# A one-core graph-attention layer with residual norm: the last four row blocks are reordered over five engines

## The chip, the cores and the metric

One core of a Trainium2 chip runs the whole kernel in one launch. The metric is device time in microseconds (us), the median over several runs; lower is better. The engines are called by their full names in the text and by the profile's names in its lines: TensorE (PE, its weight loads PEld), VectorE (DVE), ScalarE (ACT), GpSimd (POOL) and SyncE (SP). A "q" behind an engine's name in a line marks its instruction queue: waits, branches and DMA issues, in which the engine itself doesn't compute.

## The reference, cut to what matters

```python
def gnn(h, adj_mat, W, a):                 # h: 4096x512, adj_mat: 4096x4096, W: 512x2048, a: 4x1024x1
    ht = (h @ W).reshape(N, 4, 512).transpose(1, 0, 2)
    src, dst = einsum('hnd,hd->hn', ht, a_src), einsum('hnd,hd->hn', ht, a_dst)
    e = leaky_relu(src[:, :, None] + dst[:, None, :], 0.01) + adj_mat[None]
    att = softmax(e, axis=-1)
    return einsum('hij,hjd->hid', att, ht).mean(axis=0)

out = layernorm(x + gnn(x, adj, W, a))     # over the 512 columns, no weights, eps 1e-5
```

All data is float32. The entries of `adj` reach 1e9, while the scores from `src` and `dst` are small. So in nearly every row the softmax puts its whole weight on the one column where `adj` is greatest, and a row's attention output is simply that column's row of `x` times the mean of the four head matrices of `W`.

## The kernel before

The kernel uses that fact. `leading_rows` finds the greatest entry of each row of `adj`, gathers the row of `x` that it points to, multiplies it by the mean of the heads, adds the residual and normalises. It also tests for every row whether the greatest entry leads by enough for this to hold, and counts the rows where it does not; the count ends in `any_bad`. If `any_bad` is above zero, a second program part, `general`, works out the doubtful blocks in full. With these inputs it is skipped, but each engine loads `any_bad` and branches on it at its end (L61, L62).

**Tiling.** Rows are taken in NB = 32 blocks of 128. A block of `adj` is 2 MB, loaded through SyncE's DMA queue into one of six buffers. `hold` keeps all 32 blocks of `x` (128 x 32 x 512) and later, in place, the output.

**A block's way.** VectorE reduces the 4096 columns to 128 segment maxima (L163), finds the greatest segment (`find_segment`), GpSimd works out its place (`row`, L174) and gathers the 32 numbers of that segment (`lead`, L176, an indirect DMA); VectorE finds the place in it (`find_column`), GpSimd the column number (`col`, L200) and gathers the row of `x` (`y`, L186). TensorE transposes `y` (`turn`, L213), ScalarE copies it to SBUF (`yt`, L215), TensorE multiplies by `w_sum` in four 128x512 products (`products`, L228). The residual is added by one more product with the identity (`residual`, L221). Each float32 product shows in the trace as two passes. Then the row's mean and variance are taken and the block is normalised into `hold`. For the last block, 31, the segment's gather is used only for the test; its column is found by a search of the whole row (`find_column_in_row`, L206).

**Order.** All engines run in program order; a loop over t = 0 to 31 writes out a software pipeline by hand (column two steps, products three, statistics four behind the load), and a list of calls after it (lines 463 to 525) writes out the tail. Nothing is moved by a scheduler. BEHIND is 24 and LATE is 28. Blocks 0 to 23 are normalised in the loop by ScalarE (`stats`, `finish`) with the reciprocal root on GpSimd (`rstd`). The `x` of blocks 24 to 27 is loaded last, so their products are put by in SBUF (`put_by`) and added to `x` later (`add_x`, L244). Blocks 28 to 31 are measured on VectorE (`moments`: L281, L285, and a root on ScalarE, L287) and normalised by `normalise` (L297); block 31 is done in two halves of 256 columns (`products_of_half` L270, `stats_of_half` L304, `finish_in_halves`).

**The test.** `bound` (four parts, over VectorE, TensorE and ScalarE) makes a limit from the norms, `test` compares (VectorE), `count` sums over partitions by a product with ones (L394), `report` turns the sums into `n_bad` and `any_bad` (three VectorE operations, L398 to L401).

**The stores** go through SyncE's queue in program order: a store waits for its data and for one of eight completion counters to be free, and what follows in the queue waits behind it. Each store reads `hold`.

Of the kernel before, what the change touches and what calls it, by code (L numbers as in the profile page):

```python
# [10 lines left out]
U32 = mybir.dt.uint32  # L11
I32 = mybir.dt.int32
AF = mybir.ActivationFunctionType
OP = mybir.AluOpType
# [6 lines left out]
P = 128  # L21
# [45 lines left out]
def leading_rows(ctx, tc, x, adj, W, a, out, ident, v, n_bad, any_bad):  # L67
# [100 lines left out]
    def find_segment(ib):  # L168
        seg = seg_of.pop(ib)
        nc.vector.max(out=top[:, ib, :], in_=seg)  # L170
        at = small.tile([P, 8], U32, name="at")
        nc.vector.max_index(at, top[:, ib, :], seg)  # L172
        row = small.tile([P, 1], U32, name="row")
        nc.gpsimd.tensor_tensor(row, at[:, 0:1], first[:, ib : ib + 1], op=OP.add)  # L174
        lead = lead_pool.tile([P, E], F32, name="lead")
        nc.gpsimd.indirect_dma_start(  # L176
            out=lead, out_offset=None, in_=adj_segs,
            in_offset=bass.IndirectOffsetOnAxis(ap=row[:, :1], axis=0),
        )
        start = at_of[ib] = small.tile([P, 1], U32, name="start")  # L180
        nc.gpsimd.tensor_tensor(start, at[:, 0:1], width, op=OP.mult)  # L181
        lead_of[ib] = lead

    def gather_rows(ib, col):
        y = y_t[ib] = y_pool.tile([P, D], F32, name="y")
# [5 lines left out]
    def find_inner(ib):  # L191
        nc.vector.max(out=inner[:, ib, :], in_=lead_of[ib])
# [16 lines left out]
    def turn(ib):  # L209
        y = y_t.pop(ib)  # L210
        tp = psum.tile([P, KB, P], F32, name="tp", bufs=2)
        for kb in range(KB):
            nc.tensor.transpose(tp[:, kb, :], y[:, ts(kb, P)], ident)  # L213
        yt = yt_of[ib] = rows.tile([P, KB, P], F32, name="yt")
        nc.scalar.copy(yt, tp)  # L215

    def residual(ib):
        start = ib not in o_ps
        if start:
            o_ps[ib] = psum.tile([P, D], F32, name="o")  # L220
        nc.tensor.matmul(o_ps[ib], ident, hold[:, ib, :], start=start, stop=False)  # L221

    def products(ib, lo=0, hi=KB):
        start = ib not in o_ps
        if start:
            o_ps[ib] = psum.tile([P, D], F32, name="o")
        for kb in range(lo, hi):
            nc.tensor.matmul(  # L228
                o_ps[ib], yt_of[ib][:, kb, :], w_sum[:, kb, :],
                start=(start and kb == 0), stop=(kb == KB - 1),  # L230
            )
# [11 lines left out]
    def add_x(engine, ib):  # L243
        engine.tensor_add(hold[:, ib, :], hold[:, ib, :], o_ps["by"][:, ib - BEHIND, :])  # L244
        o_ps[ib] = hold[:, ib, :]

    def stats(ib):
        o, i = o_ps[ib], slice(ib, ib + 1)
        sq = rows.tile([P, D], F32, name="sq")
        nc.scalar.activation(sq, o, AF.Identity, scale=-1.0 / D, accum_out=nm[:, i])  # L250
        sq = rows.tile([P, D], F32, name="sq")
        nc.scalar.activation(sq, o, AF.Square, bias=nm[:, i], accum_out=sd[:, i])  # L252
# [6 lines left out]
    def finish(ib):  # L259
        i = slice(ib, ib + 1)  # L260
        nc.scalar.activation(hold[:, ib, :], o_ps.pop(ib), AF.Identity, bias=nm[:, i], scale=sd[:, i])  # L261

    def residual_in_halves(ib):
        o_ps[ib] = [psum.tile([P, D // 2], F32, name="o") for _ in range(2)]
        for k, o in enumerate(o_ps[ib]):
            nc.tensor.matmul(o, ident, hold[:, ib, ts(k, D // 2)], start=True, stop=False)
# [10 lines left out]
    def moments(ib):  # L277

        if ib < NB - 1:
            st = small.tile([P, nc.vector.BN_STATS_DIM], F32, name="st", bufs=2)  # L280
            nc.vector.bn_stats(st, o_ps[ib])  # L281
        else:
            st = halves_st
        mv = mean_var[ib] = small.tile([P, nc.vector.BN_AGGR_DIM], F32, name="mv", bufs=3)
        nc.vector.bn_aggr(mv, st)  # L285
        r = rt[ib] = sd[:, ib : ib + 1]
        nc.scalar.activation(r, mv[:, 1:2], AF.Sqrt, bias=eps)  # L287

    def factor(ib, shift=False):
        nc.vector.reciprocal(rt[ib], rt[ib])  # L290
        if shift:
            nc.vector.scalar_tensor_tensor(
                nm[:, ib : ib + 1], mean_var[ib][:, 0:1], -1.0, rt[ib], op0=OP.mult, op1=OP.mult
            )

    def normalise(ib, o, columns=slice(0, D)):
# [15 lines left out]
    def store(queue, lo, n):  # L312
        queue.dma_start(out_rows[:, ds(lo, n), :], hold[:, ds(lo, n), :])
# [78 lines left out]
    def count():  # L392
        pg = psum.tile([1, NB], F32, name="px", bufs=1)
        nc.tensor.matmul(pg, ones[:, 0:1], gap, start=True, stop=True)  # L394
        return pg
# [8 lines left out]
    vectors = [(kb, h) for kb in range(KB) for h in range(H)]  # L404
    vectors_at = {t: 2 if t < 3 else 1 for t in range(1, 15)}
    COLUMN, PROJECT, STATS, FINISH = 2, 3, 4, 6

    for t in range(NB):
        if t == NB // 2:
            tc.mark_branch_hint_location("general", engines=HINTED)  # L410
        if t in x_at:
            load_x(*x_at[t])
        if t + AHEAD == NB - 1:
            load_x(LATE, Q)
        load_adj(t + AHEAD)
        middle = 1 if t == NB - 1 else 2
        segment_maxima(t, 0, middle)
        if t >= COLUMN:
            find_column(t - COLUMN)
        segment_maxima(t, middle, PIECES)  # L420
        pair = FINISH <= t < BEHIND + FINISH and t % 2 == 0
        if pair:
            rstd(slice(t - FINISH, t - FINISH + 2))
        if t == NB - 1:
            for ib in (BEHIND, BEHIND + 2):
                load_x(ib, 2)
        find_segment(t)
        if t < 2:
            mean_of_heads(t)
        elif t == 2:  # L430
            mean_of_heads(2)
            mean_of_heads(3)
        if t == 0:
            turn_a()
        turned = [(*vectors[0], turn_w(*vectors.pop(0))) for _ in range(vectors_at.get(t, 0))]
        if t == 16:
            head_norms()
        ib = t - PROJECT
        if t == NB - 1:
            for late in range(LATE, NB):  # L440
                row_norm(late)
            residual(LATE)
            residual(LATE + 1)
        if ib >= 0:
            turn(ib)
            if ib > BEHIND:
                products(ib - 1, KB - 1, KB)
            if ib < BEHIND:
                residual(ib)
        for some in turned:  # L450
            head_vector(*some)
        if ib >= 0:
            products(ib, 0, KB if ib < BEHIND else KB - 1)
        if t >= BEHIND + STATS:
            put_by(t - STATS)
        elif t >= STATS:
            stats(t - STATS)
            row_norm(t - STATS)
        if pair:
            finish(t - FINISH)  # L460
            finish(t - FINISH + 1)

    for ib in range(BEHIND, LATE):
        row_norm(ib)
    for ib in range(0, 2 * Q, Q):
        store(nc.sync, ib, Q)
    for ib in range(2 * Q, BEHIND, 2):
        store(nc.sync, ib, 2)
    find_column(NB - 2)
    add_x(nc.gpsimd, BEHIND)  # L470
    add_x(nc.gpsimd, BEHIND + 1)
    find_column_in_row(NB - 1)
    add_x(nc.gpsimd, BEHIND + 2)
    products(LATE, KB - 1, KB)
    residual_in_halves(NB - 1)
    turn(NB - 3)
    products(NB - 3, 0, KB - 1)
    moments(LATE)
    for ib in range(BEHIND, NB):
        find_inner(ib)  # L480
    bound(0)
    products(NB - 3, KB - 1, KB)
    stats(BEHIND)
    factor(LATE)
    normalise(LATE, o_ps.pop(LATE))
    bound(1)
    turn(NB - 2)
    bound(2)
    add_x(nc.vector, LATE - 1)
    stats(BEHIND + 1)  # L490
    moments(LATE - 1)
    products(NB - 2, 0, 2)
    bound(3)
    test()
    pg = count()
    products(NB - 2, 2, KB - 1)
    stats(BEHIND + 2)
    rstd(slice(BEHIND, BEHIND + 2))
    rstd(slice(BEHIND + 2, BEHIND + 3))
    moments(NB - 3)  # L500
    report(pg)
    turn(NB - 1)
    factor(LATE - 1, shift=True)
    factor(NB - 3)
    normalise(NB - 3, o_ps.pop(NB - 3))
    finish(BEHIND)
    finish(BEHIND + 1)
    products(NB - 2, KB - 1, KB)
    products_of_half(NB - 1, 0)
    products_of_half(NB - 1, 1)  # L510
    nc.vector.tensor_add(hold[:, NB - 2, :], o_ps[NB - 2], hold[:, NB - 2, :])
    o_ps[NB - 2] = hold[:, NB - 2, :]
    moments(NB - 2)
    stats_of_half(NB - 1, 0)
    factor(NB - 2)
    normalise(NB - 2, o_ps.pop(NB - 2))
    finish(BEHIND + 2)
    finish(BEHIND + 3)
    stats_of_half(NB - 1, 1)
    moments(NB - 1)  # L520
    factor(NB - 1, shift=True)
    finish_in_halves(NB - 1)
    for ib, n in ((NB - 4, 1), (NB - 3, 1), (BEHIND, 2), (NB - 2, 1), (BEHIND + 2, 2)):
        store(nc.sync, ib, n)
    store(nc.sync, NB - 1, 1)

# [152 lines left out]
```

## Time and profile before

| what | value |
|---|---|
| median of 3 runs | 236.32 us (236.14 to 236.66) |
| the profiled execution | 236.21 us, of which its span (first to last instruction) is 234.6 us |
| TensorE, VectorE, ScalarE, GpSimd busy | 83%, 80%, 48%, 43% of the span |
| DMA | 97.21 MB, 414 GB/s over the span |
| mean granted TensorE clock | 0.975 |

The span begins with the first and ends with the last instruction; the execution's own time lies 1.6 us above it. The profile cuts the span into 40 slices, follows the work that ended last back as a chain, and lists groups of instructions by line, engine and tile with their durations. Times in the trace's answers are counted from the span's start.

### The profile page before, as it was taken

To read this page: it belongs to the slowest core of one execution; us is meant where nothing else is said; L and a number is where in the kernel's file an instruction comes from. 1 tells how busy PE (TensorE), PEld (TensorE's weight loads), DVE (VectorE), ACT (ScalarE), POOL (GpSimd) and SP (SyncE) were. 2 spreads that over 40 slices of the span, in tenths; PEclk is the share of its full clock that TensorE was granted. 3 is DMA by queue.
4 is the path that set the end of the run, shared out by engine and by line. 5 is a ranking of instruction groups with operands and counts; after the bars stand their busy time and mean duration, and the time that the engine had idled before them with its cause. 6 is when DMAs were issued, how large, how long until landed. Compare 5 with 4: busy or idle time off the path is not lost.

```text
span 234.6 us, 2498 instructions
## 1 busy us (share of the span) xinstructions
PE 195.2 (83%) x683; PEld 101.4 (43%) x683; DVE 188.4 (80%) x302; ACT 111.6 (48%) x267; POOL 101.2 (43%) x215
## 2 busy tenths in 40 slices
PE   0188929999999999999979879797998968698990
PEld 0034514756565655555534333242443423244460
DVE  1736875589869995999589989998799999989672
ACT  2012011255474747474758354646464645166582
POOL 1012232414527462646353645464365464549130
PEclk9999977999999999999999999999799999999998
DMA  6999999999999999999999999999999999999985
GB/s 226 439 428 426 443 425 430 415 440 412 440 420 426 424 437 434 425 424 428 427 432 433 425 433 422 432 418 429 425 432 418 422 425 427 411 425 419 417 355 210
DMA packets 13697, 97.21 MB, mean 414 GB/s; under 512 B 2152, under 2 KB 2664, under 8 KB 7792
## 3 DMA queue, kind: packets, MB, share of 16 engines
q1 hardware_dynamic: 10080, 88.08, 88.9%
q0 software_dynamic: 3584, 8.92, 9.6%
q8 instruction: 6, 0.10, 0.2%
q14 instruction: 11, 0.09, 0.1%
q10 hardware_dynamic: 16, 0.02, 0.0%
HBM read 88.62 MB, written 8.39 MB: 414 GB/s over the span
## 4 chain that ended last, share of the span: by engine, by line
DMA 45%; POOL 17%; issue 15%; PE 10%; DVE 9%; ACT 1%; POOLq 0%; SPq 0%; DVEq 0%
DMA adj_t<-in_adj_dram 42%; DVE seg L163 8%; PE o L228 7%; POOL lead L176 6%; POOL y L186 5%; DMA y<-in_x_dram,col 3%; POOL sd L256 2%; PE o L270 2%; POOL start L181 1%; POOL row L174 1%; POOL col L200 1%; PE tp L213 1%; PE o L221 1%; ACT yt L215 1%; POOL sd L255 1%
## 5 line engine op out<-in xcount | busy, mean ns | idle before, releaser
L163 DVE TENSOR_REDUCE seg<-adj_t 128x64 f32<-128x2048 f32 (+1 forms) x68 | 146.0, 2149 | 32.7 <-DMA adj_t<-in_adj_dram 32.3
L228 PE MATMUL o<-w_sum,yt 128*128 128x512 f32 x248 | 115.1, 605 | 1.7 <-ACT yt L215 1.7
L228 PEld LDWEIGHTS o<-w_sum,yt 128*128 128x128 f32 x248 | 44.5, 191 | 54.8 <-issue 42.3
L215 ACT COPY yt<-tp 128x512 f32<-128x512 f32 x32 | 18.8, 588 | 44.3 <-PE tp L213 44.3
L176 POOL DMA_INDIRECT lead<-in_adj_dram,row x32 | 32.3, 1010 | 15.5 <-POOL row L174 15.0
L186 POOL DMA_INDIRECT y<-in_x_dram,col x32 | 30.9, 965 | 15.4 <-POOL col L200 15.2
L318 PE MATMUL o<-hold,ident 128*128 128x512 f32 x32 | 18.9, 745 | 17.5 <-DMA hold<-in_L_gnn_W_dram 17.5
L213 PE MATMUL tp<-ident,y 128*128 128x128 f32 x128 | 20.0, 280 | 12.6 <-DMA y<-in_x_dram,col 12.6
L221 PE MATMUL o<-hold,ident 128*128 128x512 f32 x52 | 27.3, 611 | 0.0
L213 PEld LDWEIGHTS tp<-ident,y 128*128 128x128 f32 x128 | 14.9, 143 | 25.4 <-issue 25.0
L174 POOL TENSOR_TENSOR row<-at,first 128x1 uint32<-128x1 uint32 x32 | 6.1, 190 | 42.0 <-DVE at L172 42.0
L336 ACT COPY wt<-tp 128x512 f32<-128x512 f32 x16 | 9.2, 587 | 31.4 <-PE tp L334 31.4
L200 POOL TENSOR_TENSOR col<-start,within 128x1 uint32<-128x1 uint32 x31 | 5.9, 190 | 40.1 <-DVE within L198 40.1
L235 ACT ACTIVATE sq<-hold 128x512 f32<-128x512 f32 x32 | 19.8, 619 | 0.0
L342 PEld LDWEIGHTS pv<-at_d,wt 128*128 128x128 f32 x128 | 16.3, 191 | 6.8 <-ACT wt L336 4.0
L318 PEld LDWEIGHTS o<-hold,ident 128*128 128x128 f32 x32 | 7.4, 243 | 26.7 <-POOL row L174 11.0
L319 ACT ACTIVATE w_sum<-o 128x512 f32<-128x512 f32 x4 | 2.4, 598 | 33.9 <-PE o L318 33.9
L261 ACT ACTIVATE hold<-o,nm,sd 128x512 f32<-128x512 f32 x24 | 17.2, 771 | 0.0
L252 ACT ACTIVATE sq<-o,nm 128x512 f32<-128x512 f32 x24 | 16.5, 688 | 0.8
L342 PE MATMUL pv<-at_d,wt 128*128 128x2 f32 x128 | 15.3, 244 | 0.6 <-ACT wt L336 0.6
L250 ACT ACTIVATE sq<-o 128x512 f32<-128x512 f32 x24 | 14.6, 609 | 0.0
L334 PEld LDWEIGHTS tp<-ident,hold 128*128 128x128 f32 x64 | 7.9, 142 | 6.9 <-issue 6.9
(85 smaller groups left out, 139.8 us busy)
## 6 DMA issues: line engine op xcount, KB each, us to landing
adj_t<-in_adj_dram SPq DMA_DIRECT2D x27, 2048.0 KB, 31.3
hold<-in_x_dram SPq DMA_DIRECT2D x7, 1024.0 KB, 33.2
adj_t<-in_adj_dram SPq DMA_DIRECT2D x6, 1024.0 KB, 25.7
out_dram<-hold SPq DMA_DIRECT2D x10, 512.0 KB, 15.2
adj_t<-in_adj_dram SPq DMA_DIRECT2D x8, 512.0 KB
hold<-in_L_gnn_W_dram SPq DMA_DIRECT2D x4, 1024.0 KB
out_dram<-hold SPq DMA_DIRECT2D x2, 1024.0 KB
hold<-in_x_dram SPq DMA_DIRECT2D x2, 512.0 KB, 14.1
```

Source lines behind the costliest of these rows:

```text
L163: nc.vector.tensor_reduce(seg_of[ib][:, ts(k, S // n)], adj_t[ib][:, ts(k, N // n)].rearrange("p (s e) -> p s e", e=E), axis=AX.X, op=OP.max,)
L176: nc.gpsimd.indirect_dma_start(out=lead, out_offset=None, in_=adj_segs, in_offset=bass.IndirectOffsetOnAxis(ap=row[:, :1], axis=0),)
L186: nc.gpsimd.indirect_dma_start(out=y, out_offset=None, in_=x, in_offset=bass.IndirectOffsetOnAxis(ap=col[:, :1], axis=0),)
L213: nc.tensor.transpose(tp[:, kb, :], y[:, ts(kb, P)], ident)
L215: nc.scalar.copy(yt, tp)
L221: nc.tensor.matmul(o_ps[ib], ident, hold[:, ib, :], start=start, stop=False)
L228: nc.tensor.matmul(o_ps[ib], yt_of[ib][:, kb, :], w_sum[:, kb, :], start=(start and kb == 0), stop=(kb == KB - 1),)
L235: nc.scalar.activation(sq, hold[:, ib, :], AF.Square, accum_out=xx[:, ib : ib + 1])
L252: nc.scalar.activation(sq, o, AF.Square, bias=nm[:, i], accum_out=sd[:, i])
L261: nc.scalar.activation(hold[:, ib, :], o_ps.pop(ib), AF.Identity, bias=nm[:, i], scale=sd[:, i])
L318: nc.tensor.matmul(o, ident, hold[:, w_at + kb * H + h, :], start=(h == 0), stop=(h == H - 1))
L342: nc.tensor.matmul(pv[:, kb, h : 2 * H : H], wt[:, k, :], at_d[:, k, h : 2 * H : H], start=(k == 0), stop=(k == KB - 1),)
```

## The change

The tail is written anew; the loop and the arithmetic stay, but for the places named here.

- `find_segment` is split: the part on GpSimd is now `fetch_segment`, and for block 31 it is called after the gather of block 30's `y` and one `add_x`. The `start` of block 31 is not computed.
- Blocks 24 to 26 are normalised on GpSimd from SBUF (`finish_on_chip`), block 27 by ScalarE as before; all four `add_x` are on GpSimd.
- Block 29's residual is no longer a product, but an addition on VectorE (`add_residual`), as block 30's already was.
- On TensorE, the last product of a late block now stands between the transposes of the next and its products, and the residual of block 31 after the first matrix product of `bound`. `count` stands between the two halves of block 31.
- `report` moves from before the transposes of block 31 to after the normalising of block 30.
- `factor` uses `tensor_scalar` with two operations in place of `scalar_tensor_tensor`.
- The stores of blocks 0 to 23 are issued in the order of `HELD`, and those of the last eight blocks in the order 28, 24 and 25, 29, 26 and 27, 30, 31 (before: 28, 29, 24 and 25, 30, 26 and 27, 31).

```diff
+    def fetch_segment(ib):
+        at = at_of.pop(ib)
         row = small.tile([P, 1], U32, name="row")
...
+    def finish_on_chip(ib):
+        i, h = slice(ib, ib + 1), hold[:, ib, :]
+        o_ps.pop(ib)
+        nc.gpsimd.tensor_scalar(h, h, sd[:, i], nm[:, i], op0=OP.mult, op1=OP.add)
+
+    def add_residual(ib):
+        nc.vector.tensor_add(hold[:, ib, :], o_ps[ib], hold[:, ib, :])
+        o_ps[ib] = hold[:, ib, :]
...
+    HELD = ((8, 2), (10, 2), (0, Q), (12, 2), (14, 2), (Q, Q), (16, 2), (18, 2), (20, 2), (22, 2))
...
             residual(LATE)
-            residual(LATE + 1)
...
-    for ib in range(0, 2 * Q, Q):
-        store(nc.sync, ib, Q)
-    for ib in range(2 * Q, BEHIND, 2):
-        store(nc.sync, ib, 2)
+    for ib, n in HELD:
+        store(nc.sync, ib, n)
     find_column(NB - 2)
     add_x(nc.gpsimd, BEHIND)
-    add_x(nc.gpsimd, BEHIND + 1)
+    fetch_segment(NB - 1)
     find_column_in_row(NB - 1)
-    add_x(nc.gpsimd, BEHIND + 2)
+    for ib in (BEHIND + 1, LATE - 1, BEHIND + 2):
+        add_x(nc.gpsimd, ib)
+    turn(NB - 3)
     products(LATE, KB - 1, KB)
+    products(NB - 3, 0, KB - 1)
+    stats(BEHIND)
+    moments(LATE)
+    bound(0)
     residual_in_halves(NB - 1)
-    turn(NB - 3)
-    products(NB - 3, 0, KB - 1)
-    moments(LATE)
-    for ib in range(BEHIND, NB):
+    for ib in range(BEHIND, NB - 1):
         find_inner(ib)
-    bound(0)
-    products(NB - 3, KB - 1, KB)
-    stats(BEHIND)
+    bound(1)
     factor(LATE)
     normalise(LATE, o_ps.pop(LATE))
-    bound(1)
     turn(NB - 2)
+    products(NB - 3, KB - 1, KB)
     bound(2)
-    add_x(nc.vector, LATE - 1)
     stats(BEHIND + 1)
     moments(LATE - 1)
-    products(NB - 2, 0, 2)
+    find_inner(NB - 1)
     bound(3)
     test()
-    pg = count()
-    products(NB - 2, 2, KB - 1)
+    products(NB - 2, 0, KB - 1)
     stats(BEHIND + 2)
     rstd(slice(BEHIND, BEHIND + 2))
+    finish_on_chip(BEHIND)
+    finish_on_chip(BEHIND + 1)
     rstd(slice(BEHIND + 2, BEHIND + 3))
+    finish_on_chip(BEHIND + 2)
+    add_residual(NB - 3)
+    turn(NB - 1)
     moments(NB - 3)
-    report(pg)
-    turn(NB - 1)
     factor(LATE - 1, shift=True)
+    finish(LATE - 1)
     factor(NB - 3)
     normalise(NB - 3, o_ps.pop(NB - 3))
-    finish(BEHIND)
-    finish(BEHIND + 1)
     products(NB - 2, KB - 1, KB)
     products_of_half(NB - 1, 0)
+    pg = count()
     products_of_half(NB - 1, 1)
-    nc.vector.tensor_add(hold[:, NB - 2, :], o_ps[NB - 2], hold[:, NB - 2, :])
-    o_ps[NB - 2] = hold[:, NB - 2, :]
+    add_residual(NB - 2)
     moments(NB - 2)
     stats_of_half(NB - 1, 0)
     factor(NB - 2)
     normalise(NB - 2, o_ps.pop(NB - 2))
-    finish(BEHIND + 2)
-    finish(BEHIND + 3)
+    report(pg)
     stats_of_half(NB - 1, 1)
     moments(NB - 1)
     factor(NB - 1, shift=True)
     finish_in_halves(NB - 1)
-    for ib, n in ((NB - 4, 1), (NB - 3, 1), (BEHIND, 2), (NB - 2, 1), (BEHIND + 2, 2)):
+    for ib, n in ((LATE, 1), (BEHIND, 2), (NB - 3, 1), (BEHIND + 2, 2), (NB - 2, 1)):
         store(nc.sync, ib, n)
     store(nc.sync, NB - 1, 1)
```

More of the change, by code (lines that the diff above doesn't have):

```diff
@@ L170, in find_segment @@
         nc.vector.max(out=top[:, ib, :], in_=seg)
-        at = small.tile([P, 8], U32, name="at")
+        at = at_of[ib] = small.tile([P, 8], U32, name="at")
         nc.vector.max_index(at, top[:, ib, :], seg)
+        if ib < NB - 1:
+            fetch_segment(ib)
+    def fetch_segment(ib):
+        at = at_of.pop(ib)
         row = small.tile([P, 1], U32, name="row")
@@ L179, in find_segment @@
         )
-        start = at_of[ib] = small.tile([P, 1], U32, name="start")
-        nc.gpsimd.tensor_tensor(start, at[:, 0:1], width, op=OP.mult)
         lead_of[ib] = lead
+        if ib < NB - 1:
+            start = at_of[ib] = small.tile([P, 1], U32, name="start")
+            nc.gpsimd.tensor_tensor(start, at[:, 0:1], width, op=OP.mult)
     def gather_rows(ib, col):
@@ L291, in factor @@
         if shift:
-            nc.vector.scalar_tensor_tensor(
-                nm[:, ib : ib + 1], mean_var[ib][:, 0:1], -1.0, rt[ib], op0=OP.mult, op1=OP.mult
+            nc.vector.tensor_scalar(
+                nm[:, ib : ib + 1], mean_var[ib][:, 0:1], rt[ib], -1.0, op0=OP.mult, op1=OP.mult
             )
```

## The prediction, written before the changed kernel had run

> **What bounds the kernel now.** I read the slices first, then the chain in order of time, then the closing lines of the program, because a chain that is followed through data can miss what an engine does after its last computation.
>
> The two rows of the slices (40 of 5.87 us each; a digit is a busy share in tenths):
>
> ```profile
> POOL  1012232414527462646353645464365464549130
> DMA  6999999999999999999999999999999999999985
> ```
>
> The DMA engines are full in every slice but the first and the last two, so up to 223 us only fewer bytes could help, and the change moves none away. What is left to win or lose lies after that. The end of the chain (start, length, what):
>
> ```profile
> 203.44 0.14 issue
> 203.58 0.63 PE tp L213 x4
> ...
> 215.64 0.59 ACT yt L215
> ...
> 220.57 0.59 ACT yt L215
> ...
> 225.69 3.55 PE o L270 x16
> ...
> 230.69 0.56 ACT hold L310
> ```
>
> From the landing of the gather for block 27 (203.44) TensorE sets the pace, with short waits, to 229.24; then 2.0 us of statistics and normalising, the last store is issued at 231.29 and has landed at 233.60.
>
> Now the lines of the branch and the end, from the views of L61, L62 and L674 (durations in ns as min/median/max, then first and last start in us):
>
> ```profile
> L61 POOLq TENSOR_LOAD <-any_bad x1: 508/508/508, 225.2 to 225.2; - x1
> ...
> L62 POOLq INC_SWDGE_SEM  x1: 1476/1476/1476, 226.7 to 226.7; - x1
> ...
> L674 POOLq EVENT_SEMAPHORE  x4: 17/17/17, 233.8 to 234.5; - x4
> L674 POOLq DRAIN  x3: 40/103/5306, 228.2 to 234.3; - x3
> L674 SPq DRAIN  x3: 7/7/7, 233.7 to 234.0; - x3
> ```
>
> This is the part to see. GpSimd, whose last digit is 0, has a closing sequence of its own: it loads `any_bad` (from 225.22), takes the branch, spends 1.48 us on INC_SWDGE_SEM, then 5.31 us in a DRAIN (228.23 to 233.53): **8.31 us from the load to the end of the DRAIN**. SyncE, waiting for the last store, is through at 233.75, and the closing barrier takes 0.8 us from there. So two paths end within 0.2 us of each other, and only one is in the chain. The load needs `any_bad`, which VectorE writes early:
>
> ```profile
> 223.69 0.14 DVE L401 TENSOR_SCALAR any_bad<-total 1x1 int32<-1x1 f32 x1
> ...
> 225.25 0.19 POOL L257 TENSOR_TENSOR nm<-nm,sd 128x1 f32<-128x1 f32 x1
> ```
>
> It had been ready for 1.4 us; GpSimd's own last `rstd` (L257) let the load go.
>
> **What the Trainium skill says.** (1) "Perfetto Trace Analysis", section Sequencer-only Instruction: the profile reports such an instruction from the moment that its semaphores are satisfied to the end of execution, so waiting for a semaphore is not in it. By that, 5.31 us is work. (2) "VectorE: DVE Perf Modes", The DRAIN you can't avoid: closing DRAINs are about 12 ns on all engines. The trace agrees for SyncE (7 ns) and disagrees for GpSimd (5306 ns); the measurement decides. (3) "DMA: Bandwidth & Descriptors", Queues, rings and completion order: on each DMA engine descriptors are consumed in ring order. The trace agrees: the last five stores land in order of issue (229.05, 230.81, 231.41, 232.62, 233.60). (4) "GPSIMD Engine Reference", Elementwise: the best case is 769 ns for 512 elements, more with two inputs. The two-input L244 takes 1280 ns here; no run yet shows the large one-input operation.
>
> **The change, part by part.**
> *Store order (HELD).* The same ten stores, at 0.33 us of SyncE each, from the same full ring. The backlog was landing until 228.46, so their order alone costs 0 (bounds -0.3 to +0.3, a fifth of one 1 MB store's 2.5 us in the ring, since a gather now meets other packet sizes).
>
> *GpSimd's gathers.* The row and `lead` gather of block 31 move behind the y gather of block 30 and one add, and `start` of 31 (0.20) goes. The column of 30 is found at 210.34 as before; col 0.19, a gap of 0.54 and the issue of 0.97 end at 212.10 instead of 212.97. The add (1.28), row (0.19), a gap of 0.5 and `lead` (0.97) follow to about 215.0, so y of 31 starts at about 215.4 instead of 215.65. Landing took 6.0 to 7.3 us from the start of the issue for the last five y gathers: y of 30 at 217.1 to 218.4, y of 31 at 221.4 to 222.7 (before: 218.45, 222.74). `lead` of 31 lands near 219.5 (4.3 to 4.8 us after its issue ended, before), in time for its use near 220.
>
> *TensorE.* The residual matmul of block 29 goes: two recorded passes of 0.43 = 0.86 us. The wait for `yt` of 29 (0.68) is filled with the last product of 28, that for `yt` of 30 (0.37) with the last product of 29, and the stop for `count` (0.24) goes since `count` now stands between the halves of 31. That is 2.15 us, but the gathers take some back: the transposes of 29 would be ready at 212.35 and their data land at 213.02. From there: 0.44 transposes, 0.86 product, 2.58 three products, 0.11 for the bound, 0.86 residual halves: block 30 from 218.0 to 218.5; 0.44 + 0.86 + 0.15 + 2.58: the transposes of 31 may start at 222.1 to 222.6, its data at 221.4 to 222.7. The first product of 30 also has a new wait, for VectorE to empty the PSUM buffer of 28 (218.7 by my count, needed at 219.3 or later): 0, and behind it stands all of TensorE if I am off. I take 222.5, against 224.23 before: **1.7 us earlier**, bounds 1.1 and 2.2.
>
> *VectorE and ScalarE.* Block 29 gets an add on VectorE (0.69, as L511), but normalises from SBUF (0.55 instead of 0.81); the add of 27 (0.67) leaves VectorE, and its statistics wait for GpSimd until about 218.9, behind which stand the test and block 29. These end near 221.3 and 225, ahead of the last product of 30 and roughly level with it: nothing. The factor's other operation: 0.16 to 0.16, nothing. ScalarE loses three `finish` (0.75 each), which lay beside TensorE: nothing.
>
> *GpSimd's normalising (finish_on_chip).* Three operations of 128x512: 0.77 (the skill's best case) to 1.28 (L244) each; I take 1.1. With `rstd` of 24 and 25 from about 220.8 (1.27 us), GpSimd's last one is dispatched near 225.3 and ends near 226.5. SyncE stands at the store of 24 and 25 until about 224.3, with 29 and all later ones behind; their ring is still full until 225.3 to 228.5, so nothing. The later stores come 1 to 3 us sooner and fill pauses of the ring. The last store could then land near 232.8: 228.46 plus seven blocks at 0.62 us (two blocks took 1.24). **This path alone gains 0.8 us.**
>
> *The report of `any_bad`.* It was written at 223.83, before TensorE's last 5.4 us. Now it stands in VectorE's queue behind the sum, statistics and normalising of block 30. From the transposes of 31 (222.5): 0.44 + 0.86 + 0.17 to the end of the last product of 30; 0.69 add, 0.70 + 0.18 statistics; the half of 31 is ready then, 0.43; reciprocal 0.16, normalising 0.55; the report's three operations 0.45, with gaps some 0.35: **any_bad at about 227.5**. GpSimd's load waits for it: 225.22 becomes 227.5, the DRAIN ends at 227.5 + 8.31 = 235.8, against 233.53 (its gather count, and I assume its length, unchanged). The barrier adds 0.8: the span is 236.65 instead of 234.6, **2.05 us longer**. The profiled execution took 236.21 with that span, and the median is 0.11 above it: 236.32 + 2.05 = 238.4.
>
> Behind the moved wait, on GpSimd, stands only its closing sequence; all engines wait for that in the barrier.
>
> **The rivals.**
> *B, faster.* The DRAIN is not 5.3 us of work but ends with something else: the last store's 15th of 16 completions is at 233.52, the DRAIN's end at 233.53. Then a later `any_bad` costs nothing, as long as GpSimd reaches the DRAIN (about 230.7) before the last store lands, and SyncE's path decides: 0.8 us less, 235.5. For it speaks that coincidence; against it, that the DRAIN waits on no semaphore and that the skill leaves waits out of the span. It decides if the DRAIN is under about 2.2 us when entered at 230.7.
> *C, no change.* As B, but y of 31 lands a microsecond later than I take it, or SyncE's wait for GpSimd holds stores back beyond the backlog: TensorE's gain is gone, 236.2.
> *D, slower still.* As forecast, with a gather of 31 that is a microsecond late: `any_bad` follows it one for one, 239.5.
> *E, half.* The change brings `any_bad` sooner than I think, by GpSimd's last dispatch at 225.3 alone: 236.4 to 237.
>
> **How the numbers follow.** Forecast 0.77 (238.4; 237.4 to 239.2 from the bounds on block 31), B 0.12, C 0.03, D 0.05, E 0.03. The range 236.9 to 239.4 leaves out B, C and some of D and E. What a measurement here can tell from no change is about 0.2% (0.47 us): faster 0.12, within 0.2% 0.04, slower 0.84. Since slower holds most of this, the range stays on that side.
>
> **What would show it.** Right: in the views of L61 and of the closing lines (L687 after the change) GpSimd's load starts near 227.5 instead of 225.2 and its DRAIN near 230.5, again 5.3 us long, and SyncE's wait for the last store is over 2 to 3 us before the barrier; TensorE's last half ends near 227.7 instead of 229.24. Wrong: the DRAIN shrinks as it is entered later (B), or TensorE's end has not moved (C), or the load starts well before 227 (E).

## The result, and the profile after

| | before | after |
|---|---|---|
| median | 236.38 us (235.87 to 236.87, 6 runs) | 239.7 us (238.97 to 241.51, 6 runs) |
| ratio, with its 95% interval | 1 | 1.0154 (1.0113 to 1.0196) |
| the profiled execution | 236.21 us, span 234.6 | 239.84 us, span 238.2 |

The change makes the kernel 3.3 us slower. The forecast was 238.4, with a range to 239.4: the right direction, but too small by 1.3 us. Every profile is of one execution, and these reach the tail at different times (the gather of block 27 is issued at 196.17 us before, at 196.46 after, and between 195.97 and 199.91 in the experiments). Those of e1 and g2 were among the longest runs of their kernels, so of these two the order and the durations are read and the ends are not.

The slices of the page, after:

```profile
POOL 1012322326535643645254636463556465448710
DMA  6999999999999999999999999999999999999971
```

GpSimd's last three digits were 1, 3 and 0 and are 7, 1 and 0: the slice with the 7 (220.3 to 226.3) holds the end of its adds, the roots, and the first two of the three normalisings which it has taken over. In the DMA row the last digit has fallen from 5 to 1: the last store has landed at 234.24, 4 us before the end, while before it landed at 233.60, one us before the end. So the end no longer hangs on bytes. On what it hangs, the views of the branch and of the closing lines tell (ns as min/median/max, then first and last start in us; L687 was L674):

```profile
L61 POOLq TENSOR_LOAD <-any_bad x1: 500/500/500, 229.1 to 229.1; - x1
...
L62 POOLq INC_SWDGE_SEM  x1: 1476/1476/1476, 230.6 to 230.6; - x1
...
L687 POOLq EVENT_SEMAPHORE  x4: 17/17/17, 237.4 to 238.1; - x4
L687 POOLq DRAIN  x3: 40/103/5306, 232.1 to 237.9; - x3
L687 SPq DRAIN  x3: 7/7/7, 234.3 to 237.6; - x3
```

Every duration of GpSimd's closing sequence is what it was, 1476 and 5306 ns, and the whole sequence has moved: the load from 225.22 to 229.06, the end of the DRAIN from 233.53 to 237.37. That is 8.31 us from the load to the end of the DRAIN, the same as before. SyncE is through with the last store at 234.38 (233.75 before) and now stands for 3.0 us. Before, the two paths ended 0.2 us apart.

VectorE's timeline of the changed kernel says why the load is late (start, length, line, out<-in):

```profile
228.12 0.55 DVE L312 TENSOR_SCALAR hold<-hold,mv,sd 128x512 f32<-128x512 f32 x1
...
228.89 0.14 DVE L416 TENSOR_SCALAR any_bad<-total 1x1 int32<-1x1 f32 x1
```

`any_bad` is written at 229.03, behind the normalising of block 30, and GpSimd's load follows 0.03 us later.

The chain of the changed kernel, in order of time, stays blind to all this: it ends with the last block's data (it counts a step from the end of the one before, so block 31's transposes stand at 223.99 here and at 223.83 in TensorE's timeline further below).

```profile
212.03 7.26 DMA y<-in_x_dram,col
...
219.42 0.63 PE tp L219 x4
...
223.99 0.44 PE tp L219 x4
...
227.25 1.94 PE o L285 x8
...
229.21 0.44 DVE halves_st L319
...
230.69 0.56 ACT hold L325
```

A reader who trusts the chain alone sees work that ends at 231.25, as it did before, and no reason for 3.6 us more.

### The profile page after: what moved, and what is told of

Its sections match the earlier page's. It is cut to its first block, busy times and chain, and to the rows that moved or that the text cites. A ratio compares the mean times of both kernels' runs of the same rounds, so it can differ in the third digit from the quotient of the medians.

```text
span 238.2 us, 2493 instructions
## 1 busy us (share of the span) xinstructions
PE 196.6 (83%) x681; PEld 101.1 (42%) x681; DVE 188.0 (79%) x302; ACT 109.5 (46%) x264; POOL 104.2 (44%) x218
## 4 chain that ended last, share of the span: by engine, by line
DMA 45%; issue 19%; POOL 19%; DVE 9%; PE 4%; ACT 0%; POOLq 0%; SPq 0%; DVEq 0%
DMA adj_t<-in_adj_dram 42%; DVE seg L163 7%; POOL lead L181 6%; POOL y L192 6%; DMA y<-in_x_dram,col 3%; PE o L234 2%; POOL sd L262 2%; PE o L285 2%; POOL start L188 1%; POOL row L179 1%; POOL col L206 1%; POOL sd L261 0%; DVE at L172 0%; PE tp L219 0%; DVE top L170 0%
## 5 line engine op out<-in xcount | busy, mean ns | idle before, releaser
L234 PE MATMUL o<-w_sum,yt 128*128 128x512 f32 x248 | 116.7, 612 | 0.7 <-ACT yt L221 0.7
L234 PEld LDWEIGHTS o<-w_sum,yt 128*128 128x128 f32 x248 | 45.3, 194 | 55.0 <-issue 43.1
```

Source lines behind the costliest of these rows:

```text
L234: nc.tensor.matmul(o_ps[ib], yt_of[ib][:, kb, :], w_sum[:, kb, :], start=(start and kb == 0), stop=(kb == KB - 1),)
```

## The experiments

All ratios are to the kernel before, timed beside it, with a 95% interval. Theory 1 is the forecast's: the loss is the late `report`, by way of GpSimd's fixed closing sequence. Its main rivals are that the new order of stores, or the work that GpSimd has taken over, makes the loss.

**e3: the kernel before, with only `report` moved.**

```diff
     moments(NB - 3)
-    report(pg)
...
     normalise(NB - 2, o_ps.pop(NB - 2))
+    report(pg)
```

> The kernel before with the call of report alone moved from ahead of the transposes of block 31 to behind the normalising of block 30; count stays. Closing-sequence theory: any_bad is written near 229.1 instead of 223.8, GpSimd's load starts there instead of at 225.2, the DRAIN ends near 237.4: span 238.3, 239.9 us, the whole loss of the change from one moved call. Rival (the DRAIN ends with the last store, and the loss is elsewhere): 236.4.

Measured: 239.6 us, ratio 1.0137 (1.0092 to 1.0181), 4 runs. The views of L61 and of the closing lines of e3:

```profile
L61 POOLq TENSOR_LOAD <-any_bad x1: 510/510/510, 229.6 to 229.6; - x1
...
L674 POOLq DRAIN  x3: 40/103/5306, 232.7 to 238.5; - x3
L674 SPq DRAIN  x3: 7/7/7, 235.0 to 238.2; - x3
```

One moved call, with its three short operations, is enough for the whole loss: the load moves to 229.64 and the 5306 ns DRAIN follows, unchanged. No other part of the change is in this kernel.

**e1: the changed kernel with `count` and `report` early.** `count` goes ahead of the transposes of block 31, `report` behind the `factor` of block 27.

```diff
     add_residual(NB - 3)
+    pg = count()
     turn(NB - 1)
     moments(NB - 3)
     factor(LATE - 1, shift=True)
+    report(pg)
...
-    pg = count()
...
-    report(pg)
```

> The changed kernel with count moved ahead of the transposes of block 31 and report moved to just behind the factor of block 27, nothing else. Closing-sequence theory (GpSimd's way from its load of any_bad to the end of its DRAIN is 8.31 us of fixed work): any_bad is written near 224.9 instead of 229.0, the load is then let go by GpSimd's own last finish_on_chip near 226.4, the DRAIN ends near 234.7: 237.1 us, so 2.6 us of the 3.3 lost come back. Rival (the rest of the new tail is what costs, by later gathers and stores): no more than 0.5 us comes back, 239.2 to 239.7.

Measured: 237.53 us, ratio 1.0041 (1.0005 to 1.0078), 8 runs. 2.2 of the 3.3 us are back (239.7 against 237.53), where 2.6 were expected. What is left fits GpSimd's own queue, as e1's trace shows (VectorE's and GpSimd's timeline, then the view of L61):

```profile
226.77 0.14 DVE L416 TENSOR_SCALAR any_bad<-total 1x1 int32<-1x1 f32 x1
...
228.61 0.77 POOL L272 TENSOR_SCALAR hold<-hold,sd,nm 128x512 f32<-128x512 f32 x1
...
L61 POOLq TENSOR_LOAD <-any_bad x1: 779/779/779, 228.6 to 228.6; - x1
```

`any_bad` has been ready for 1.6 us when the load starts, together with `finish_on_chip` of block 26, the last one in the same queue; and beside it the load takes 779 ns in place of 500.

**e2: e1, and blocks 24 to 26 normalised by ScalarE again.**

```diff
-    finish_on_chip(BEHIND)
-    finish_on_chip(BEHIND + 1)
...
-    finish_on_chip(BEHIND + 2)
...
-    finish(LATE - 1)
+    for ib in (BEHIND, BEHIND + 1, LATE - 1, BEHIND + 2):
+        finish(ib)
```

> As e1_report_early, and blocks 24 to 26 are normalised by ScalarE's finish instead of finish_on_chip, so GpSimd ends with rstd. Closing-sequence theory: the load is let go near 225 to 225.5, the DRAIN ends by 233.8, and SyncE's wait for the last store decides: 235.8 to 236.6, level with the kernel before. Rival (late gathers and stores): 239 or more.

Measured: 236.4 us, ratio 0.9998 (0.9973 to 1.0024), 20 runs. The closing lines of e2:

```profile
L61 POOLq TENSOR_LOAD <-any_bad x1: 504/504/504, 225.4 to 225.4; - x1
...
L685 POOLq DRAIN  x3: 40/103/5306, 228.4 to 234.8; - x3
L685 SPq DRAIN  x3: 7/7/7, 234.2 to 234.5; - x3
```

The load is back at 225.41 and GpSimd is done at 233.72, before SyncE (234.2). The loss is gone. The rest of the change, with TensorE's new order and the new orders of stores in it, is worth nothing that can be measured: the interval allows 0.6 us either way.

**f3: the kernel before, with the order of `HELD` alone.**

```diff
-    for ib in range(0, 2 * Q, Q):
-        store(nc.sync, ib, Q)
-    for ib in range(2 * Q, BEHIND, 2):
-        store(nc.sync, ib, 2)
+    for ib, n in ((8, 2), (10, 2), (0, Q), (12, 2), (14, 2), (Q, Q), (16, 2), (18, 2), (20, 2), (22, 2)):
+        store(nc.sync, ib, n)
```

> The kernel before with the new order of the stores of blocks 0 to 23 (HELD) alone. Forecast of the change: order costs 0, bounds 0.3 us either way, 236.3. Rival (the order delays the gathers): y of 28 and 30 land a microsecond later in the profile and the time rises to 237 or more.

Measured: 236.32 us, ratio 0.9988 (0.9969 to 1.0008), 22 runs. The order of the early stores costs nothing that can be measured (at most 0.2%), as the forecast had it.

**e4: what the DRAIN's length hangs on.** The kernel before, with 14 gathers more: a second one beside the `lead` gather of 14 blocks, with the same rows, into tiles that nobody reads.

```diff
+    EXTRA = 14
...
         lead_of[ib] = lead
+        if ib % 2 == 0 and ib < 2 * EXTRA:
+            spare = once.tile([P, E], F32, name=f"spare{ib}")
+            nc.gpsimd.indirect_dma_start(
+                out=spare, out_offset=None, in_=adj_segs,
...
```

> The kernel before with a second copy of the lead gather into a spare tile in 14 of the 32 blocks (0, 2, .. 26), so 78 indirect DMAs on GpSimd instead of 64. If the closing DRAIN works through the program's indirect DMAs, it takes 5306 x 78/64 = 6470 ns instead of 5306, and INC_SWDGE_SEM perhaps more than 1476; the time rises by about 1 us, to 237.4. If its length is fixed, 5306 ns and 236.4 to 236.8. If it ends with the last store, its end stays within 0.1 us of that landing whatever its start.

One execution: 238.41 us. Its closing lines:

```profile
L61 POOLq TENSOR_LOAD <-any_bad x1: 507/507/507, 226.2 to 226.2; - x1
...
L62 POOLq INC_SWDGE_SEM  x1: 1756/1756/1756, 227.7 to 227.7; - x1
...
L681 POOLq DRAIN  x3: 40/103/6449, 229.5 to 236.5; - x3
L681 SPq DRAIN  x3: 7/7/7, 234.6 to 236.2; - x3
```

With 78 indirect DMAs in place of 64 the DRAIN takes 6449 ns, against 5306 × 78/64 = 6467: 82 to 83 ns for each gather of the whole program. INC_SWDGE_SEM grows by 280 ns, 20 ns for each one added. The DRAIN ends at 235.94, 1.4 us after the last store has landed (234.56), so it does not end with that store.

**f4 and g1: a DRAIN midway, in the kernel before.**

```diff
+    DRAIN_AT = 16
...
         find_segment(t)
+        if t == DRAIN_AT:
+            nc.gpsimd.drain()
```

> The kernel before with one DRAIN on GpSimd behind find_segment of step 16, by which 32 or so of the 64 gathers have been issued. If the DRAIN works through the gathers issued since the last one, at 5306/64 = 83 ns each, the closing DRAIN falls to about 2.6 us and the one in the middle takes about 2.6 us and waits for the gathers under way besides; the closing DRAIN's end moves from 233.5 to about 231 and the last store alone decides. If it works through all gathers of the program whatever was drained, the closing one stays at 5306 ns. The pause of GpSimd in the middle may delay VectorE; the time itself is not forecast better than 236 to 240.

One execution, f4: 235.98 us. The view of the added line (L430), then of the closing lines:

```profile
L430 POOLq DRAIN  x1: 7655/7655/7655, 122.4 to 122.4; - x1
...
L677 POOLq DRAIN  x3: 46/103/2677, 227.4 to 234.1; - x3
L677 SPq DRAIN  x3: 7/7/7, 233.5 to 233.8; - x3
```

The closing DRAIN has halved, 2677 of 5306 ns, when half of the gathers lie ahead of another DRAIN. So it works through the gathers issued since the last one, and GpSimd is done at 230.08. The added DRAIN takes 7655 ns at 122 us (8194 in g1), where about 2.6 us and the landing of gathers under way were expected; that it is longer may be that landing, which was not tried by itself.

> The kernel of f4_drain_midway again, timed in rounds. In its profile GpSimd was through at 230.1 instead of 233.5 and SyncE's wait for the last store decided alone. If GpSimd's closing DRAIN was a second bound of the kernel before in part of its runs, the time falls by 0.1 to 0.2%, 235.9 to 236.2; if the last store alone decided, 236.4.

Measured on the same kernel over more executions, g1: 236.33 us, ratio 1.0015 (0.999 to 1.0039), 14 runs. With GpSimd's path 3 us shorter the kernel before gains nothing: SyncE's last store sets its end alone, and the pause of some 8 us in GpSimd's queue midway costs nothing that can be seen.

**g2: the changed kernel with the same DRAIN midway.** `report` stays where the change put it.

> The changed kernel with one DRAIN on GpSimd behind find_segment of step 16 and nothing else; report stays late. The closing DRAIN falls from 5306 to about 2680 ns and INC_SWDGE_SEM from 1476 to about 840, so GpSimd is through 3.2 us after what it was, near 234.1, level with the last store at 234.2: 236.4 to 236.9 us, nearly the whole loss back with any_bad as late as before. If something else in the late report costs, 239 or more.

Measured: 236.73 us, ratio 1.0031 (1.0009 to 1.0052), 22 runs, against 1.0154 without it. Its views of L61, L62 and the closing lines:

```profile
L61 POOLq TENSOR_LOAD <-any_bad x1: 506/506/506, 231.1 to 231.1; - x1
...
L62 POOLq INC_SWDGE_SEM  x1: 836/836/836, 232.6 to 232.6; - x1
...
L690 POOLq DRAIN  x3: 46/103/2677, 233.5 to 237.2; - x3
```

DRAIN and INC_SWDGE_SEM are shorter by 2.63 and 0.64 us, 3.27 together, and the median falls by 3.0. Of the loss 0.3% is left. A late `any_bad` costs little when the sequence behind it is short. This shows the mechanism from its other side: it is lateness and length together that made the loss.

**f1: the changed kernel, with the instruction fetches moved.** The profile lists a queue of 16 KB packets as one that brings in instructions (the last section tells what it does to a gather). To see whether that made the forecast's missing microsecond, 33 tiny products were put into TensorE's program in steps 4 to 14, which shifts where in time those packets fall.

```diff
+    PADS = range(4, 15)
...
+        if t in PADS:
+            px = psum.tile([1, NB], F32, name="px", bufs=1)
+            for _ in range(3):
+                nc.tensor.matmul(px, ones[:, 0:1], ident[:, :NB], start=True, stop=True)
         if pair:
```

> The changed kernel with 33 tiny TensorE products (ones times 32 columns of the identity, result unread), three in each of the steps 4 to 14, so that TensorE's 16 KB instruction fetches fall at other places of the program; the steps have TensorE idle time. Fetch theory (the fetch near 206 us holds one DMA engine for 0.94 us, and the 16th part of the y gather then under way lands 1.2 to 1.5 us after the other 15; that is what put the transposes of 31 at 223.8 instead of the 222.5 of the forecast): with no fetch between 200 and 222 us no gather of the tail has such a straggler, block 28's gather lands near 207.9, any_bad is written near 227.7, 238.2 to 238.6 us. Rival (the gathers are late because of the new store order or the full ring): nothing changes, 239.7.

Measured: 238.97 us, ratio 1.0096 (1.0072 to 1.012), 6 runs: 0.7 us less than the changed kernel, half to two thirds of what was expected of it, and the two intervals (1.0113 to 1.0196 without the added products) overlap a little, so the times alone don't prove a gain. TensorE's timeline of f1, the transposes of blocks 28, 30 and 31 (in brackets the wait and who ended it):

```profile
207.53 0.63 PE L220 MATMUL tp<-ident,y 128*128 128x128 f32 x4 [0.28 <-DMA y<-in_x_dram,col]
...
217.85 0.60 PE L220 MATMUL tp<-ident,y 128*128 128x128 f32 x4
...
223.05 0.63 PE L220 MATMUL tp<-ident,y 128*128 128x128 f32 x4 [0.66 <-DMA y<-in_x_dram,col]
```

Blocks 28 and 30 are now in time, with the wait for block 30 gone. But a fetch falls at 221.8, onto the gather of block 31, of which 15 parts had landed at 222.02 and the last at 222.91. `any_bad` comes at 228.29, 0.74 us sooner than in the changed kernel, in place of the 1.1 to 1.5 hoped for; and this execution had issued the gather of block 27 at 195.97, 0.49 us sooner, so that less than half of the 0.74 was won in the tail.

**f2, g3, g4: is there a version that beats both?** f2 is e2 with the added products, g3 is e2 with the DRAIN midway, g4 is f2 with the DRAIN midway.

> e2_early_scalar with the same 33 tiny TensorE products as f1_after_pad. Fetch theory: TensorE's last half ends near 228 instead of 229.5, the last store is issued near 230.3, and the time is set by the ring of stores and GpSimd's DRAIN (233.7 before): 235.4 to 235.8, 0.2 to 0.4% below the kernel before. Rival (late gathers have another cause): 236.4, as e2_early_scalar.

Measured, f2: 236.53 us, ratio 0.9996 (0.9979 to 1.0012), 22 runs.

> e2_early_scalar with the DRAIN in the middle. GpSimd's closing is then off the path by 3 us or more; what is left is the last store: 236.0 to 236.4 if the ring of stores and the late gathers decide, as I now hold; 235.5 or less if GpSimd's closing still bounded e2_early_scalar.

Measured, g3: 236.47 us, ratio 1.0011 (0.9987 to 1.0035), 14 runs.

> f2_early_scalar_pad with the DRAIN in the middle: no instruction fetch on a gather of blocks 28 to 30 and GpSimd's closing short. In f2_early_scalar_pad TensorE ended 0.8 us sooner than in the kernel before and the time was still 236.5, because the last store landed 3.2 us after its issue behind a full ring. Ring theory: 236.0 to 236.5, no better. Rival (GpSimd's closing held f2_early_scalar_pad back): 235.5.

Measured, g4: 236.8 us, ratio 1.0022 (1.0004 to 1.0039), 22 runs.

None gains; f2 was expected at 235.4 to 235.8 and g4 at 236.5 at most, and both are above that. In f2 TensorE ends at 228.45, 0.8 us sooner than before, and its last store is issued at 230.63 instead of 231.29. It lands at 233.84 (before: 233.60): 3.2 us after its issue, where it took 2.3 before. The windows of f2 (length, busy us of TensorE, its weight loads, VectorE, ScalarE and GpSimd, then granted clock, DMA share, GB/s):

```profile
226.00:228.00 2.00, 2.00 (x11) 1.77 (x10) 1.53 (x5) 1.87 (x4) 0.00 (x0) 1.00 0.72 290
228.00:230.00 2.00, 0.45 (x3) 0.04 (x1) 1.53 (x7) 0.29 (x1) 0.00 (x0) 1.00 1.04 410
230.00:232.00 2.00, 0.00 (x0) 0.00 (x0) 0.46 (x2) 0.56 (x1) 0.00 (x0) 0.65 0.78 301
```

The 16 engines are full between 228 and 230 (the DMA share of the kernel before is 0.79 there), so the stores come closer together. That is not what holds the last one: 15 of its 16 parts have landed at 232.96, 2.3 us after the issue and 0.56 us sooner than before (233.52). The last part comes 0.88 us behind them. One engine was late from the stores ahead on: 15 of the 16 parts of block 30's store had landed at 231.91, the last at 233.23. A fetch of 0.88 us began at 229.6; the trace does not say on which engine it ran, so that it made this engine late is likely and not shown. Whether the end of this ring can be brought forward was not tried further.

## Why the prediction was right or wrong

**The mechanism: right.** The forecast said that GpSimd's closing sequence is fixed at 8.31 us and that `any_bad` would start it late. It is 8.31 us after the change, and e3 makes the loss with the one moved call, e1 takes two thirds of it away by moving the call back, e2 all of it by freeing GpSimd's queue besides, and g2 takes most of it away by shortening the sequence.

**Rival B: refuted.** The DRAIN kept its 5306 ns when it was entered at 232.07 in place of 228.23, and e4 and f4 show what it is: 83 ns per gather since the last DRAIN. That its end lay 0.01 us beside a completion of the last store was chance. The sentence of the Trainium skill's "Perfetto Trace Analysis" on Sequencer-only Instruction (the span begins when the semaphores are satisfied) was the right ground to doubt that coincidence. Rival D, `any_bad` late one for one with a gather, was the nearest, though the gather was block 30's and not block 31's.

**The term that was mis-sized: the start of block 31's transposes.** The forecast took 222.5, from sums that gave 222.1 to 222.6; its stated bounds, 1.1 to 2.2 us sooner than before, are wider than these sums and reach to 223.1. The trace has 223.83, and from there to `any_bad` 5.2 us in place of 5.0. That is 1.33 + 0.2 = 1.5 us, and the span grew by 3.6 in place of 2.05. TensorE's timeline of the changed kernel, blocks 28 to 31:

```profile
209.45 0.63 PE L219 MATMUL tp<-ident,y 128*128 128x128 f32 x4 [1.76 <-DMA y<-in_x_dram,col]
...
213.60 0.63 PE L219 MATMUL tp<-ident,y 128*128 128x128 f32 x4
...
219.42 0.63 PE L219 MATMUL tp<-ident,y 128*128 128x128 f32 x4 [0.71 <-DMA y<-in_x_dram,col]
...
223.83 0.60 PE L219 MATMUL tp<-ident,y 128*128 128x128 f32 x4
```

The wait that ends last ahead of block 31 is the one for block 30's `y`. It landed at 219.29, where the forecast had bounds of 217.1 to 218.4. The step that failed stands at the start of that reckoning: "the column of 30 is found at 210.34 as before". VectorE waits there for block 30's `lead`, and GpSimd issues `y` after it (first the kernel before, then the changed one):

```profile
210.08 0.09 DVE L198 MATCH_VALUE_LOAD within<-top,lead 128x8 f32 x1 [0.45 <-DMA lead<-in_adj_dram,row]
...
210.89 0.09 DVE L204 MATCH_VALUE_LOAD within<-top,lead 128x8 f32 x1 [0.96 <-DMA lead<-in_adj_dram,row]
...
212.03 0.96 POOL L192 DMA_INDIRECT y<-in_x_dram,col  x1 [0.60 <-POOL col L206]
```

- `lead` landed at 210.80 (before: 209.99), so the column was found at 211.16, and the issue of `y` began at 212.03 where 211.13 was forecast. GpSimd's own steps between were as forecast to 0.1 us, and the 7.26 us from there to the landing lie within the forecast's 6.0 to 7.3. So `y` is out of its bounds by the lateness of `lead`.
- Of that lateness 0.29 us is the execution's, which stood that much behind already when `lead` was issued (204.75 against 204.46). The rest is its last part: 15 of its 16 parts were there at 210.01. A 16 KB fetch had begun at 206.20. In the seven profiles with such a fetch at 206.0 to 207.8, this last part is 0.28 to 0.79 us behind the 15th; in the seven without, 0.03 to 0.13. The forecast had taken its landings from one execution of the kernel before, whose fetch lay on block 27. In e3, f3, f4, g1 and e4, which leave TensorE's program as it was, it lay on block 28 too, so this lateness is not shown to come from the change; the change made it count, by putting `any_bad` behind block 30.
- The same fetch lay on block 28's gather, with 15 parts at 207.79 and the last at 209.32. Block 28's transposes began at 209.45, where the forecast's sums imply 208.47: in the kernel before they began at 209.33, behind block 29's residual of 0.86 us, and without it TensorE now stood idle. This 1.76 us is TensorE's longest wait in the tail and cost nothing by itself: TensorE was through with all that comes ahead of block 30's transposes at 218.7 and waited for block 30 in any case.
- From block 30 to block 31 TensorE took 4.41 us in place of 4.03, with no wait recorded.

Block 31's own `y` was not far from deciding: it landed at 222.92 (bounds 221.4 to 222.7). The forecast let its issue begin at 215.4, and overlooked that it follows the end of the column's search by 0.8 us (214.84 to 215.65 before, 215.65 to 216.41 after), and the search starts behind block 30's column.

f1 bears the reading out. With no fetch on block 28, `lead` of block 30 has all its parts at 209.47, the last 0.03 us behind; block 31's transposes stand ready at 223.05 - 0.66 = 222.39, and a fetch on block 31 itself keeps them to 223.05. Counted from the issue of block 27's gather, that is ready after 26.4 us, against 26.3 in the forecast and 27.4 in the changed kernel. The forecast's bounds treated a landing as a matter of the ring alone; by the trace one sixteenth of a gather can be held up for a microsecond by something that the program does not write down.

**VectorE's part, and ScalarE's: not nothing for `any_bad`.** The 5.2 us after block 31's transposes are close to the forecast's 5.0 by luck, since two errors in it nearly cancel. VectorE began to add block 30 at 225.94, 0.64 us later than the last product allowed by the forecast's sum (225.30), and was then 0.42 us quicker over the rest. It was still at block 29, waiting for its root:

```profile
225.28 0.16 DVE L305 RECIPROCAL sd<-sd 128x1 f32<-128x1 f32 x1 [0.87 <-ACT sd L302]
225.47 0.55 DVE L312 TENSOR_SCALAR hold<-hold,mv,sd 128x512 f32<-128x512 f32 x1
225.94 0.68 DVE L275 TENSOR_TENSOR hold<-o,hold 128x512 f32<-128x512 f32 x1
```

In the new order `turn` of block 31 is called ahead of `moments` of block 29, so in ScalarE's queue the root stands behind the copy of block 31's transposes. This is read from the trace of one execution and was not tried by itself. Where `any_bad` does not stand behind it, in e2, it costs nothing that can be measured.

**TensorE 1.5 us sooner, and the store path 0.8 us ahead: wrong in the changed kernel, and without value where it came nearer.** TensorE ends at 229.17 (229.24 before, 227.7 forecast): the pauses were filled, but 1.76 and 0.71 us of waits took their place. That TensorE's end has not moved was the sign named for rival C, and of C this half came true; the total did not follow it, since GpSimd's path was the longer one. In f2 TensorE does end 0.8 us sooner, and 15 of the 16 parts of the last store are there at 232.96, near the forecast's 232.8; the sixteenth, at 233.84, takes the gain away.

**GpSimd's normalising: dispatched later, but shorter.** GpSimd's timeline of the changed kernel:

```profile
223.60 1.52 POOL L272 TENSOR_SCALAR hold<-hold,sd,nm 128x512 f32<-128x512 f32 x2
...
226.43 0.77 POOL L272 TENSOR_SCALAR hold<-hold,sd,nm 128x512 f32<-128x512 f32 x1
```

Each takes 0.77 us, the lower bound (in f1 the last took 1.03); the 769 ns that the Trainium skill's "GPSIMD Engine Reference", Elementwise, gives as the best case was the value to take, not 1.1. The last one begins at 226.43, where 225.3 was forecast. By itself this work is not free: in e1, where `report` is early, it is what holds the load, and e2 gains 1.1 us (237.53 to 236.4) without it. In the changed kernel it hides behind the later `any_bad`.

**Store orders at nothing: right** (f3 for `HELD`; e2, with both orders, for the rest).

## What to carry to other kernels

Look at what each engine still has to do after its last computation, in the views of the branch and of the closing lines, before calling a small bookkeeping step free: here a value of 4 bytes, written 5.2 us later, cost 3.3 us, because it opened an 8.3 us sequence that no chain of data shows. Let the value that an engine branches on be ready early, and keep that engine's queue short ahead of the branch. When a program issues many gathers from GpSimd, count the 83 ns for each that were measured here into its end, or drain once midway where GpSimd has time to spare. When two engines' paths end within some tenths of a microsecond of each other, as here, shortening one of them alone gains nothing (g1).

## What the runs showed of the hardware that was not expected

**GpSimd's closing DRAIN is a bill for its gathers:** 5306 ns for 64, 6449 for 78, 2677 for the half after a DRAIN midway; INC_SWDGE_SEM ahead of it took 1476, 1756 and 836 ns.

**Fetching instructions delays data.** The page of the changed kernel lists it among the DMA queues (packets, MB, share of 16 engines):

```profile
q8 instruction: 6, 0.10, 0.2%
```

Six packets of 16 KB in the whole program look like nothing. But each takes 0.9 to 1.2 us, and when one falls into the wait for a gather, the last of its 16 parts comes late, while a gather is only done with its last part. The landings of the 15th and 16th part of a `y` gather with such a fetch under way, in us: before, fetch at 201.2: 202.25 and 203.44; after, 206.2: 207.79 and 209.32; e1, 211.6: 213.45 and 214.88; e3, 206.7: 208.28 and 209.79; g2, 218.6: 220.19 and 221.31; f1, 221.8: 222.02 and 222.91. Of the 14 profiles all but f2's, which has no fetch between 200 and 225, have one `y` gather among blocks 27 to 31 whose last part is behind in this way, by 0.80 to 1.55 us. Of the gathers from block 26 on, those with no such packet under way have it 0.0 to 0.5 us behind, but for block 31's, where it is up to 0.79 (221.95 and 222.74 before) with a packet of 8 KB of the queue q14, also called instruction, under way. That the fetch sits on the late part's engine is inferred; the trace does not name the engine.

What sets the place of the fetch stays open. The added products of f1 moved it, but in e3, f3, f4, g1 and e4, where TensorE's program is that of the kernel before, it came at 206.0 to 207.8 and not at 201.2. So an edit that changes no wait can move a landing by a microsecond.
